# Layer 3's experts by slots: results written straight to the tokens' places, weights kept, weights spread by exact products

## The chip, the core and the metric

The kernel runs on one NeuronCore of a Trainium2 chip, as one launch. The metric is the device time of the launch in microseconds. Five engines work side by side, each through its own instructions in order: TensorE (PE in the profile; its weight loads are PEld), VectorE (DVE), ScalarE (ACT), GpSimd (POOL) and SyncE (SP), which here only issues DMA transfers. POOL issues DMA transfers too: those that cast, and the indirect ones, in which every row has an index of its own.

## The reference, cut to what matters

A decoder of four layers runs on `x` of shape (4, 512, 128). Each layer has an attention, a cross attention over 77 context rows, and a feed-forward part. The change lies in the last part, layer 3's mixture of experts:

```
logits = X @ gate_w.T;  scores = sigmoid(logits)
idx = top_k(scores + bias, 4);  w = scores[idx] / sum
pos = running count of each expert's tokens, over all tokens in order
valid = pos < 128                      # C = 2 * 512 * 4 // 32
xe[expert, pos] = X                    # 32 experts x 128 slots
ye = (silu(xe @ W1) * (xe @ W3)) @ W2  # 128 -> 64 -> 128
out = sum over the 4 choices of ye[expert, pos] * w   (0 where not valid)
out = out + (silu(X @ sw1.T) * (X @ sw3.T)) @ sw2.T   # a shared expert
x = x + out
```

Each expert has 128 slots in all. A token that comes after its expert is full gets nothing from it.

## The kernel before

`x` stays in SBUF as 16 tiles of 128 tokens by 128 channels, four tiles a batch, with `xn` (normalized rows) and `xT` (normalized, channels by tokens). Stages are Python generators. `weave` steps a dense stage and, between its steps, a second chain; the framework then orders each engine's instructions and adds the semaphores. Pools give tiles; a tile with `bufs=n` has n buffers, and the writer of the next one waits until the readers of the one n before are done. PSUM has eight banks, shared out by `banks(...)`: in the last stage four `f`, one `acc`, three `s`.

Layer 3's end, in the order of the program:

- **The cross attention** (`l3_xattn`, 32 items of a batch and a pair of heads) goes through `lagged`: in a round each phase works on another item (projections, scores, values, turn). The softmax division is a POOL operation (L527). Woven into it are the norms and, for batches 0 to 2, `route_slots`: `capped` routes and counts places; from that come `to` (the slot of each token and choice, or a number out of range), `back` (the same, clamped to 0 or more) and `wk` (the weight). Sixteen indirect DMAs a batch on POOL (L749) then write the token's `xn` rows to `slots` in DRAM, 32 x 128 rows of 128 channels, cleared beforehand (`empty_slots`). POOL works in order, so a softmax division behind them waits.
- **The shared expert** of batches 0 to 2 (`shared_rows`).
- **The rounds** (`slot_experts`): eight rounds of four experts. All eight slot tiles are fetched by SP at once (L782), as soon as the last slot write has landed. A round turns the slots (`turn`), multiplies gate and up (`inner`), turns the inner rows (`inner_turn`) and multiplies down (`down`). PSUM is copied to `made` (three buffers; ScalarE L827, VectorE L828), which SP writes to DRAM (L829).
- Beside these, batch 3 is normalized and routed by `route_dense`. `spread` turns its weights and writes them to DRAM as `l_ffn_w`.
- **The dense block** (`ffn` for batch 3): 17 units (the shared expert, then 16 pairs of experts with 64 inner channels each). A unit is gate and up (PE L417, two banks `f`), silu on ScalarE (L939), `h` times up and `h` times the spread weight `c` on VectorE (L428), and down (PE L947), issued two units later and summed in `acc`. `c` is read back from `l_ffn_w` by SP, each row broadcast to 64 partitions (L911).
- **The gathers** (`gathered`), woven into the dense block: 48 indirect DMAs on POOL (L860), 16 a batch, each reading 128 rows of `made` by `back`; VectorE adds each, times `wk`, to `x` (L866); `store` writes the batch out.
- The dense sum is turned and added to `x`, and batch 3 is written out.

The experts' weights are six packs of up to three units, cast while loaded, from POOL (L369). They pass through `feed`, a list of packs for the kernel's four weight buffers (`want(i)` loads up to entry i); the rounds and the dense block each load all six.

Of the kernel before, what the change touches and what calls it, by code (L numbers as in the profile page):

```python
# [130 lines left out]
def pack_all(inp):  # L131
# [6 lines left out]
    p.add("tri4", rep((np.arange(4)[None, :] < np.arange(4)[:, None]).astype(f32)))  # L138
    p.add("slot1", rep((np.arange(32) * CAP + 1).astype(f32)))
# [149 lines left out]
class Net:  # L289
# [7 lines left out]
    def __init__(self, ctx, tc, packs, dram, feed):  # L297
        self.tc, self.nc = tc, tc.nc
        self.packs, self.dram = packs, dram
        self.feed, self.loaded = feed, []  # L300
        self.turn = 0
# [75 lines left out]
    def pack(self, i, name):  # L377
        assert self.feed[i] == name, (self.feed[i], name)
        self.want(i)
        return self.loaded[i]  # L380
# [23 lines left out]
    def lagged(self, items, *phases):  # L404

        for r in range(len(items) + max(lag for _, lag in phases)):
            for phase, lag in phases:
                if 0 <= r - lag < len(items):
                    phase(*items[r - lag])
            yield  # L410
# [298 lines left out]
    def route_dense(self, b, W, pool):  # L709

        m = {}
        yield from self.capped(b, W, pool, m)
        yield
        yield from self.spread(m["w"], (b,), self.weights_in("l3_ffn", 32), pool)

    def route_slots(self, b, W, pool):
# [18 lines left out]
        to, back, none = own([P, TB, K], I32, "to"), own([P, TB, K], I32, "back"), one([P, TB, K], "none")  # L735
        nc.vector.tensor_scalar(none, top, 0.0, 2.0 * E * CAP, ALU.is_equal, ALU.mult)
        nc.vector.scalar_tensor_tensor(to, top, -1.0, none, ALU.add, ALU.add)
        nc.vector.tensor_scalar(back, top, -1.0, 0.0, ALU.add, ALU.max)
        yield
        same, wk = one([P, TB, K, E], "same"), own([P, TB, K], F32, "wk")  # L740
# [3 lines left out]
        nc.vector.tensor_reduce(wk, same, AX.X, ALU.add)  # L744
        self.placed[b] = back, wk
        for t in range(TB):
            for k in range(K):

                put = nc.gpsimd.indirect_dma_start(  # L749
                    out=self.slots, out_offset=bass.IndirectOffsetOnAxis(ap=to[:, t, k : k + 1], axis=0),  # L750
                    in_=self.xn[:, TB * b + t, :], in_offset=None, bounds_check=E * CAP - 1, oob_is_err=False,
                )
                self.tc.declare_no_dep(put.ins, group="slots", reason="rows of their own")
                self.tc.add_to_no_dep_group("slots", put.ins)
            yield

    def empty_slots(self, pool):

        E = 32
        self.slots = self.away.tile([E * CAP, D], F32, name="slots")  # L760
        self.made = self.away.tile([E * CAP, D], F32, name="made")
        self.placed = {}
        none = pool.tile([P, 8 * D], F32, name="none", bufs=1)
        self.nc.gpsimd.memset(none, 0.0)
        rows = self.slots.rearrange("(g p n) d -> g p (n d)", p=P, n=8)
        for g in range(4):
            self.nc.sync.dma_start(rows[g], none)

    def slot_experts(self, base, pool):
# [7 lines left out]
        back = self.made.rearrange("(e c) d -> c e d", c=CAP)  # L777
        xs, st = {}, {}

        def fetch(q):  # L780
            xs[q] = pool.tile([P, 4, D], F32, tag="slots", name="slots", bufs=8)
            nc.sync.dma_start(xs[q], by_expert[:, 4 * q : 4 * q + 4, :])  # L782

        def turn(q):
            t = self.bank("f", (P, 4, P))
            for e in range(4):
                nc.tensor.transpose(t[:, e, :], xs[q][:, e, :], self.ident)
# [4 lines left out]
        def inner(q):  # L792
            ps = self.bank("f", (P, 4, 2, H))
            xT = st.pop((q, "xT"))
            for e in range(4):
# [6 lines left out]
                if e == 3:  # L802
                    self.want(base + i + 2)
# [5 lines left out]
        def inner_turn(q):  # L809
            h = st.pop((q, "h"))  # L810
            t = self.bank("s", (P, 2, P))
# [6 lines left out]
        def down(q):  # L818
# [8 lines left out]
            nc.scalar.copy(y[:, :, 0, :], ps[0])  # L827
            nc.vector.tensor_copy(y[:, :, 1, :], ps[1])  # L828
            nc.sync.dma_start(back[:, 4 * q : 4 * q + 4, :], y.rearrange("p k h d -> p (k h) d"))  # L829
# [4 lines left out]
        yield from self.lagged([(q,) for q in range(8)], (inner, 1), (down, 3), (inner_turn, 2), (turn, 0))  # L834

# [17 lines left out]
    def gathered(self, b, pool):  # L853

        nc = self.nc
        back, wk = self.placed.pop(b)
        for t in range(TB):
            g = pool.tile([P, 4, D], F32, tag="back", name="back", bufs=8)
            for k in range(4):
                nc.gpsimd.indirect_dma_start(  # L860
                    out=g[:, k, :], out_offset=None, in_=self.made,
                    in_offset=bass.IndirectOffsetOnAxis(ap=back[:, t, k : k + 1], axis=0),
                )
            x = self.x[:, TB * b + t, :]
            for k in range(4):
                nc.vector.scalar_tensor_tensor(x, g[:, k, :], wk[:, t, k : k + 1], x, ALU.mult, ALU.add)  # L866
            yield
        self.store(b)
# [23 lines left out]
    def ffn(self, stage, group, E, base, pool):  # L892
# [5 lines left out]
        away = self.chunks[stage]  # L898
# [3 lines left out]
        def chunk():  # L902

            if not rest:
# [16 lines left out]
        for k, blk in enumerate(blocks):  # L921
# [3 lines left out]
            for b in group:  # L925
# [4 lines left out]
                acc = {}  # L930
                for i, (W, u, in_c) in enumerate(plan):
                    if in_c == 0:
                        chunk()
                        c = coming.pop(0)
# [6 lines left out]
                    if in_c is not None:  # L941
                        self.tt(h, h, c[:, in_c, :], ALU.mult)
# [1163 lines left out]
def build(nc, packs, dram):  # L2106
# [5 lines left out]
    for name, part in (  # L2112
        ("l0a", of("l0_ffn")), ("l0b", of("l0_ffn")), ("l1a", of("l1_ffn")), ("l1b", of("l1_ffn")),
        ("l2", f2 + f2), ("x3", ["l3_xattn.q"]), ("l3a", of("l3_ffn")), ("l3b", of("l3_ffn")),
# [3 lines left out]
    with tile.TileContext(nc) as tc, ExitStack() as ctx:  # L2118
# [133 lines left out]
        net.weave(some(steps, 12), chained(net.norm(1), net.norm(2), net.norm(3)), 1)  # L2252
        net.weave(some(steps, 8), chain5(0), 0.41)
        net.want(at["l3a"] + 1)
        net.weave(some(steps, 8), chain5(1), 0.41)
        net.weave(steps, chain5(2), 0.41)
# [6 lines left out]
        banks(f=4, acc=1, s=3)  # L2263
        chain = chained(net.norm(3), net.route_dense(3, W5, s5))
# [29 lines left out]
```

## Time and profile before

| what | value |
|---|---|
| time, median of 3 runs | 2357.78 us (2355.03 to 2363.65) |
| time of the profiled execution | 2353.91 us |
| its span, first to last instruction | 2352.1 us |
| mean granted TensorE clock | 0.96 |
| busy: PE, DVE, ACT, POOL | 2192.3, 1605.1, 1034.3, 572.7 us |
| slot writes `slots<-xn` (POOL), first to last issue | 2102.2 to 2209.5 us |
| slot fetches (SP) | from 2211.6 us |
| gathers `back<-made` (POOL), first to last issue | 2256.6 to 2329.1 us |
| last operation on `x` (DVE) | 2348.0 us |

Positions are microseconds from the start of the span. A timeline line has start, duration, engine, source line, operation, what it writes and reads, and in brackets the idle time before it with what released it; several like operations in a row are one line with xN. An fp32 product over 512 columns stands as two MATMUL records. A line of waits has who waited, for whom, the sum in us, how many times, and the longest. A line of windows has the stretch, its length, each engine's busy time with its instructions, the granted clock as a share, the DMA engines' share and GB/s. Most small helpers carry one source line for all their callers (L417 every product, L428 every two-operand VectorE operation), so the tile's name tells more than the line.

### The profile page before, as it was taken

What the parts mean: (1) busy time and instruction counts of PE and PEld (TensorE: products, weight loads), DVE (VectorE), ACT (ScalarE), POOL (GpSimd) and SP (SyncE); (2) the same over time, 40 slices, a digit from 0 to 9 for tenths busy, and PEclk for the clock granted to TensorE, in tenths of its full rate; (3) what the DMA queues carried; (4) which work ended last, traced back from release to release, by engine and by line L of the source; (5) the groups of instructions that cost most, each with busy time, mean ns of one, the idle gap of its engine ahead of it and who ended that gap; (6) DMA issues with size and microseconds to landing.
All of it is one profiled execution on the core that took longest, in us unless ns stands there. A gap on an engine that the chain in (4) does not pass through costs nothing.

```text
span 2352.1 us, 28673 instructions
## 1 busy us (share of the span) xinstructions
PE 2192.3 (93%) x9282; PEld 1156.3 (49%) x9282; DVE 1605.1 (68%) x4051; ACT 1034.3 (44%) x2105; POOL 572.7 (24%) x712
## 2 busy tenths in 40 slices
PE   6999899999999998999999999999999985999865
PEld 3566556555545453444444444444444443666531
DVE  6677574766766687878777787767767756776433
ACT  4555546434335543444444434444444443455310
POOL 1000001000000103333323333323333322346343
PEclk8998999999999999999999999999999997999887
DMA  5321242354353342333333334333333360000287
GB/s 165 95 69 32 85 124 78 87 131 114 95 148 80 100 104 74 83 92 89 106 91 83 107 104 107 101 91 96 106 91 82 99 127 36 1 6 1 72 161 71
DMA packets 84144, 210.95 MB, mean 90 GB/s; under 512 B 18873, under 2 KB 41721, under 8 KB 83661
## 3 DMA queue, kind: packets, MB, share of 16 engines
q1 hardware_dynamic: 79050, 198.99, 32.0%
q0 software_dynamic: 4944, 10.14, 3.6%
q8 instruction: 73, 1.20, 0.2%
q14 instruction: 77, 0.63, 0.1%
HBM read 179.76 MB, written 20.23 MB: 85 GB/s over the span
## 4 chain that ended last, share of the span: by engine, by line
PE 74%; DVE 13%; issue 4%; DMA 3%; POOL 3%; ACT 2%; another core or an unknown queue 0%; SPq 0%; POOLq 0%; ACTq 0%; DVEq 0%
PE mm L417 21%; PE f L417 12%; PE mm L1783 8%; PE s L417 8%; PE acc L947 5%; PE mm L1750 5%; PE mm L1733 4%; DMA back<-made,back 3%; PE acc L2077 2%; DVE h L428 2%; PE mm L1115 1%; PE mm L1137 1%; DVE m L1077 1%; PE mm L1070 1%; PE s L507 1%
## 5 line engine op out<-in xcount | busy, mean ns | idle before, releaser
L1694 POOL TENSOR_TENSOR gvx<-gvx 128x512 f32<-128x512 f32 (+1 forms) x256 | 260.1, 1016 | 583.1 <-DVE gvx L428 527.9
L417 PE MATMUL f<-xT,w_l_ffn 128*128 128x512 f32 (+1 forms) x768 | 374.9, 610 | 13.4 <-DVE h L428 12.7
L417 PE MATMUL mm<-w_l_ffn_qkv,xT 128*128 128x512 f32 x512 | 265.4, 603 | 3.3 <-DVE roped L1665 1.7
L1814 ACT ACTIVATE at_e<-mm,at_m 128x512 f32<-128x512 f32 x256 | 173.0, 685 | 215.1 <-DVE at_m L1812 209.3
L1783 PE MATMUL mm<-og,w_l_ffn_o 128*128 128x512 f32 x512 | 264.6, 600 | 0.0
L939 ACT ACTIVATE h<-f 128x512 f32<-128x512 f32 x189 | 112.5, 596 | 289.3 <-PE f L417 253.4
L947 PE MATMUL acc<-h,w_l_ffn 128*128 128x512 f32 x378 | 200.5, 616 | 30.1 <-issue 10.3
L417 PEld LDWEIGHTS f<-xT,w_l_ffn 128*128 128x128 f32 (+1 forms) x768 | 141.5, 194 | 168.9 <-issue 130.0
L428 DVE TENSOR_TENSOR h<-h,f 128x512 f32<-128x512 f32 (+1 forms) x192 | 131.4, 686 | 130.4 <-PE f L417 99.2
L428 DVE TENSOR_TENSOR og<-mm,c 128x512 f32<-128x512 f32 x256 | 175.9, 688 | 29.0 <-PE mm L1783 27.6
L428 DVE TENSOR_TENSOR gvx<-mm,gv 128x512 f32<-128x512 f32 x256 | 174.4, 683 | 23.6 <-PE mm L417 18.9
L1734 ACT COPY eT<-mm 128x512 f32<-128x512 f32 x256 | 137.7, 595 | 72.9 <-PE mm L1733 72.6
L1812 DVE TENSOR_REDUCE at_m<-mm 128x1 f32<-128x512 f32 x256 | 161.2, 683 | 8.7 <-PE mm L417 7.0
L1733 PEld LDWEIGHTS mm<-ident,at_e 128*128 128x128 f32 x1024 | 120.0, 141 | 67.0 <-issue 49.4
L1783 PEld LDWEIGHTS mm<-og,w_l_ffn_o 128*128 128x128 f32 x512 | 89.4, 191 | 97.0 <-issue 85.3
L1733 PE MATMUL mm<-ident,at_e 128*128 128x128 f32 x1024 | 134.1, 273 | 2.6 <-ACT at_e L1814 2.6
L417 PE MATMUL mm<-roped 64*128 64x512 f32 x512 | 133.3, 623 | 1.5 <-DVE roped L428 1.0
L947 PEld LDWEIGHTS acc<-h,w_l_ffn 128*128 128x128 f32 x378 | 71.6, 196 | 125.5 <-issue 81.4
L417 PEld LDWEIGHTS mm<-w_l_ffn_qkv,xT 128*128 128x128 f32 x512 | 86.7, 190 | 91.9 <-issue 69.4
L1077 DVE TENSOR_REDUCE m<-mm 128x1 f32<-128x512 f32 (+3 forms) x176 | 105.2, 637 | 31.9 <-PE mm L1073 31.0
L428 DVE TENSOR_TENSOR h<-h,c 128x512 f32<-128x512 f32 x176 | 121.4, 696 | 4.2 <-DMA c<-l_ffn_w 1.1
L1750 PE MATMUL mm<-eT,v 128*64 128x512 f32 x512 | 119.5, 599 | 0.0
(440 smaller groups left out, 3672.1 us busy)
## 6 DMA issues: line engine op xcount, KB each, us to landing
c<-gates SPq DMA_DIRECT2D x256, 256.0 KB
c<-l_ffn_w SPq DMA_DIRECT2D x106, 384.0 KB
w_l_ffn<-in_l_ffn SPq DMA_DIRECT2D x26, 576.0 KB
w_l_ffn_qkv<-in_l_ffn_qkv SPq DMA_DIRECT2D x16, 640.0 KB
w_l_ffn_o<-in_l_ffn_o SPq DMA_DIRECT2D x16, 512.0 KB
rot<-qk SPq DMA_DIRECT2D x128, 64.0 KB
w_l_ffn<-in_l_ffn POOLq DMA_DIRECT2D x10, 576.0 KB
k_parts<-k SPq DMA_DIRECT2D x12, 384.0 KB
```

Source lines behind the costliest of these rows:

```text
L417: self.nc.tensor.matmul(out, lhsT=lhsT, rhs=rhs, start=i == 0, stop=i == len(pairs) - 1)
L428: self.nc.vector.tensor_tensor(out, a, b, op)
L939: nc.scalar.activation(h, pg, AF.Silu)
L947: nc.tensor.matmul(acc["t"], lhsT=W["d" + u], rhs=h, start=i == 0, stop=i == n - 1)
L1077: nc.vector.tensor_reduce(m[:, i, h0 : h0 + per], ps, AX.X, ALU.max, negate=True)
L1694: nc.gpsimd.tensor_tensor(x[:, :, :m], x[:, :, :m], x[:, :, m : 2 * m], ALU.add)
L1733: nc.tensor.transpose(p[:, j, :], es[i][hl][:, j * P : j * P + P], self.ident)
L1734: nc.scalar.copy(eT[hl][:, :, i * P : i * P + P], p)
L1750: nc.tensor.matmul(po[64 * hl : 64 * hl + 64, :], lhsT=m["v"][:, j, hl, :], rhs=eT[hl][:, j, :], start=j == 0, stop=j == TB - 1,)
L1783: nc.tensor.matmul(acc, lhsT=W["o"][:, (e - 1) * D : e * D], rhs=hs.pop(e - 1), start=e == 1, stop=e == E)
L1812: nc.vector.tensor_reduce(m, s, AX.X, ALU.max, negate=True)
L1814: nc.scalar.activation(e[:, :n], s, AF.Exp, bias=m, accum_out=den)
```

## The change

- A slot row has 130 columns: the token's row, its weight, and its place (token times 4 plus choice) as an integer. `sent` (one buffer) is filled by ScalarE copies, a VectorE reduction (the weight) and an addition (the place), and the 16 indirect writes a batch send its rows. Unused slots carry weight 0 and a place out of range.
- In a round, the down results are multiplied by the slots' weight as they leave PSUM (two operations on each of ScalarE and VectorE instead of one), and four indirect DMAs on POOL write them to the tokens' places in `back` (6144 rows in DRAM, cleared beforehand). Instead of the 48 gathers, `returned` reads one block a batch by SP and adds four operands of 128x512 to `x`.
- Batch 3's weights are split into three bf16 parts whose sum is the fp32 value, turned, and kept in SBUF (`w3T`). Each unit's spread weight is a bf16 product of `pick3`, zeros and ones, with `w3T` into an `s` bank (`spread3`), which VectorE reads in place of `c`. No DRAM round trip is left.
- The six weight packs are loaded once: three through the feed, three into the last stage's pool (`stay`).
- `inner_turn` takes an `f` bank instead of an `s` bank. `lagged` yields after each phase instead of each round, and the weaves' paces are changed to match. In the dense block VectorE keeps the program's order.

```diff
@@ lagged
                     phase(*items[r - lag])
-            yield
+                    yield
@@ route_dense
-        yield from self.spread(m["w"], (b,), self.weights_in("l3_ffn", 32), pool)
+        w3, rest = pool.tile([P, TB, 3, E], BF16, ...), pool.tile([P, TB, E], F32, ...)
+        nc.vector.tensor_copy(w3[:, :, 0], m["w"])
+        self.tt(rest, m["w"], w3[:, :, 0], ALU.subtract)
+        nc.vector.tensor_copy(w3[:, :, 1], rest)
+        self.tt(w3[:, :, 2], rest, w3[:, :, 1], ALU.subtract)
+        yield
+        t = self.bank("s", [3 * E, S], BF16)
+        for j in range(TB):
+            nc.tensor.transpose(t[:, j * P : j * P + P], w3[:, j].rearrange("p k e -> p (k e)"), self.identb)
+        self.w3T = pool.tile([3 * E, S], BF16, name="w3T", bufs=1)
+        nc.scalar.copy(self.w3T, t)
@@ route_slots
-        nc.vector.tensor_scalar(back, top, -1.0, 0.0, ALU.add, ALU.max)
+        sent = pool.tile([P, TB, K, D + 2], F32, name="sent", tag="sent", bufs=1)
+        for t in range(TB):
+            nc.scalar.copy(sent[:, t, :, :D], self.xn[:, TB * b + t, :].unsqueeze(1).to_broadcast([P, K, D]))
+        nc.vector.tensor_scalar(
+            sent[:, :, :, D + 1].bitcast(I32), self.const["place"].rearrange("p (t k) -> p t k", k=K),
+            float(b * S * K), None, ALU.add,
+        )
...
-        nc.vector.tensor_reduce(wk, same, AX.X, ALU.add)
-        self.placed[b] = back, wk
+        nc.vector.tensor_reduce(sent[:, :, :, D], same, AX.X, ALU.add)
...
-                    in_=self.xn[:, TB * b + t, :], in_offset=None, ...
+                    in_=sent[:, t, k, :], in_offset=None, ...
@@ empty_slots
+        self.back = self.away.tile([3 * S * K, D], F32, name="back")
+        rows = pool.tile([3 * E, E], F32, name="own_rows", bufs=1)
+        self.pick3 = pool.tile([3 * E, E, 64], BF16, name="pick3", bufs=1)
...
+        self.nc.gpsimd.tensor_copy(self.pick3, rows.unsqueeze(2).to_broadcast([3 * E, E, 64]))
...
+        nowhere = none[:, :, D + 1]
+        self.nc.vector.tensor_scalar(nowhere.bitcast(I32), nowhere, float(1 << 20), None, ALU.add)
...
+        for g in range(6):
+            self.nc.sync.dma_start(rows[g], zero)
@@ slot_experts
-            t = self.bank("s", (P, 2, P))
+            t = self.bank("f", (P, 2, P))
...
-            nc.scalar.copy(y[:, :, 0, :], ps[0])
-            nc.vector.tensor_copy(y[:, :, 1, :], ps[1])
-            nc.sync.dma_start(back[:, 4 * q : 4 * q + 4, :], y.rearrange("p k h d -> p (k h) d"))
+            for k in range(2):
+                w = [xs[q][:, 2 * k + half, D : D + 1] for half in range(2)]
+                nc.scalar.activation(y[:, k, 0, :], ps[0][:, k, :], AF.Copy, scale=w[0])
+                nc.vector.tensor_scalar(y[:, k, 1, :], ps[1][:, k, :], w[1], None, ALU.mult)
+                for half in range(2):
+                    self.alone("back", nc.gpsimd.indirect_dma_start(
+                        out=self.back, in_=y[:, k, half, :], in_offset=None,
+                        out_offset=bass.IndirectOffsetOnAxis(
+                            ap=xs[q][:, 2 * k + half, D + 1 : D + 2].bitcast(I32), axis=0
+                        ),
+                        bounds_check=3 * S * 4 - 1, oob_is_err=False,
+                    ))
...
+    def spread3(self, units):
+        out = {}
+        for u in units:
+            out[u] = self.bank("s", (P, S))
+            at = 2 * int(u)
+            self.dot(out[u], (self.pick3[:, at : at + 2, :].rearrange("r e i -> r (e i)"), self.w3T))
+        return out
@@ gathered -> returned
+        for b in batches:
+            rows[b] = pool.tile([P, TB, 4, D], F32, name=f"back{b}", bufs=1)
+            src = self.back[b * S * 4 : (b + 1) * S * 4].rearrange("(t p k) d -> p t k d", p=P, k=4)
+            self.nc.sync.dma_start(rows[b], src)
+        yield
+        for b in batches:
+            x = self.rows_of(self.x, b)
+            for k in range(4):
+                self.tt(x, x, rows[b][:, :, k, :], ALU.add)
+                if k % 2:
+                    yield
+            self.store(b)
@@ ffn
+                    if in_c is not None and spread:
+                        if u not in cs:
+                            cs.update(spread([v for _, v, in_c in plan[i : i + 2] if in_c is not None]))
+                        cu = cs.pop(u)
...
-                        self.tt(h, h, c[:, in_c, :], ALU.mult)
+                        self.tt(h, h, cu, ALU.mult)
@@ build
-        net.weave(some(steps, 8), chain5(0), 0.41)
-        net.want(at["l3a"] + 1)
-        net.weave(some(steps, 8), chain5(1), 0.41)
-        net.weave(steps, chain5(2), 0.41)
+        net.weave(some(steps, 32), chain5(0), 1.7)
+        net.want(at["l3"] + 1)
+        net.weave(some(steps, 32), chain5(1), 1.7)
+        net.weave(steps, chain5(2), 1.15)
...
+        net.want(at["l3"] + 2)
+        for i, n in enumerate(of("l3_ffn")):
+            net.stay[n] = net.loaded[at["l3"] + i] if i < 3 else net.load(n, ff, f"w{i}")
...
-        net.weave(chained(shared, net.slot_experts(at["l3a"], ff)), chain, 1.2)
-        back = chained(*[net.gathered(b, ff) for b in range(3)])
-        net.weave(net.ffn("l3_ffn", (3,), 32, at["l3b"], ff), back, 1, 2)
+        net.weave(chained(shared, net.slot_experts(at["l3"], ff)), chain, 2.2)
+        with tc.manual_schedule(engines={mybir.EngineType.DVE}):
+            back = net.returned(range(3), ff)
+            next(back)
+            net.weave(net.ffn("l3_ffn", (3,), 32, at["l3"], ff, net.spread3), back, 1.5, 6)
```

## The prediction

> **What bounds the kernel now.** I read first where the span has holes, then what ends last, then each hole's releaser. The page's slices (58.8 us each):
>
> ```profile
> PE   6999899999999998999999999999999985999865
> ...
> PEclk8998999999999999999999999999999997999887
> DMA  5321242354353342333333334333333360000287
> ```
>
> TensorE is full almost everywhere; the last two slices (2234 to 2352) hold 6 and 5 tenths at a lowered clock, while the DMA engines, idle before, go to 8 and 7 tenths. The change works only in the last 340 us. The waits in 2250:2341 say what the holes are:
>
> ```profile
> ACT h L939 <- PE f L417: 63.1, 12, 15.5
> DVE x L866 <- DMA back<-made,back: 54.2, 30, 11.9
> ```
>
> ScalarE's 63.1 us only follow TensorE. VectorE waits 54.2 us for gathered rows, 30 times. It works in program order, so each wait also holds the dense block's `h` products behind it, and TensorE for free banks. The chain of waits cut to 2240:2352.1 puts 54.4% on "DMA back<-made,back". How fast the dense block goes when fed shows in TensorE's timeline:
>
> ```profile
> 2291.74 1.02 PE L947 MATMUL acc<-h,w_l_ffn 128*128 128x512 f32 x2
> 2292.60 1.88 PE L417 MATMUL f<-xT,w_l_ffn 128*128 128x512 f32 x4
> 2294.32 1.02 PE L947 MATMUL acc<-h,w_l_ffn 128*128 128x512 f32 x2
> 2295.18 1.88 PE L417 MATMUL f<-xT,w_l_ffn 128*128 128x512 f32 x4
> ```
>
> From one `acc` to the next is 2294.32 - 2291.74 = 2.58 us: 1.72 for gate and up, 0.86 for down. Seventeen units are 43.9 us, yet the block runs from about 2249 to 2346. So half of it is waiting.
>
> Why are gathers slow and index writes not? The DMA answer for 2189:2211 holds 16 writes `slots<-xn`:
>
> ```profile
> DMA packets 481, 0.03 MB, mean 1 GB/s; under 512 B 480, under 2 KB 480, under 8 KB 480
> ```
>
> Sixteen writes of 128 rows by 512 B would be 1.05 MB; 0.03 went. Nearly all rows were out of range (their experts' 128 slots were already full) and cost the DMA nothing. A gather cannot skip: `back` is clamped to row 0 or more. In 2320:2330 the engines are 97% busy at 66 GB/s. The 48 gathers take from 2256.6 to about 2341, 1.76 us each.
>
> **Part by part.**
>
> *Gathers go* (L860, L866): 48 x 0.98 us on POOL, 48 x 0.35 us on VectorE, and the waits. *The spread of batch 3's weights goes:* the chain has the write of `l_ffn_w` (2249.48 to 2253.41), SP's issue (0.46) and 2.72 for `c`; with it go twelve transfers `c` and the eight writes of `made` from SP. In its place stand four small VectorE operations (0.2 to 0.3 us by `wf` and cast rows), four bf16 transposes (0.23) and one copy (0.57), all issued among the rounds: nothing on the path. *Weights stay:* the old second load goes, six loads. The three new pool tiles are issued on POOL behind batch 2's writes (order of instructions) and share DMA with the slot fetch, which moves 2.11 MB by about 2220; three loads at some 2 us of all engines end near 2227, and the first is needed at round 3 (2229 before). Zero, at most 3.
>
> *Spread products come:* 16 bf16 matmuls of 512 columns. Bounds: 0.22 (half of the fp32 product's two 0.43 records) to 0.50 (the old `mm<-turned,pick` row). I take 0.25, since the block is warm when fed: a unit is 2.83 us.
>
> *`sent` and the slots' rows:* three times four ScalarE copies of 128x512, 0.6 us each (the `xT` row), 2.4 per batch; ScalarE is under half busy there (9.51 of 20 in 2100:2120). The first must wait for all 16 writes of the batch before (one buffer), and ScalarE's `xT`, `q`, exponentials and `eT` queue behind it, and so TensorE. In time before, batch 0's writes leave POOL at 2125.2 and `xT` comes at 2128.2; batch 1's at 2170.6 and 2173.6: about 3 us of cover. If it goes, ScalarE stands for what is late: three writes are 3.8 us, so up to 4 us per batch. The first write now also needs the weights' sum:
>
> ```profile
> 2189.52 0.17 DVE L737 SCALAR_TENSOR_TENSOR to<-m,none 128x16 int32<-128x16 f32 x1
> 2189.64 0.69 DVE L428 TENSOR_TENSOR same<-same,wf 128x512 f32<-128x512 f32 x1
> 2190.37 0.69 DVE L744 TENSOR_REDUCE wk<-same 128x16 f32<-128x512 f32 x1
> ```
>
> 2191.06 instead of 2189.69, for batch 2, whose 16 writes end the stage: +1.4. I put +1.5 on everything after. The finer weave of this stage (a step per phase) has the same total; it can win back at most the 7 us that TensorE idles in 2080:2180, or lose as much. I take zero. The new POOL work of the clearing (two memsets of 0.97, one bf16 copy, between 0.6 and 4.2 us by the `pick` and `kb` rows) falls in POOL's hole from 1959 to 1990, the six more clears in an idle DMA.
>
> *The rounds.* `made` becomes two smaller operations on each engine: VectorE +0.28 per round (0.35 row), ScalarE +0.45 (0.41, `xn` row); both have over 1 us free per 3.3 us round. New on POOL are 32 index writes. Their price by the nearest rows:
>
> ```profile
> 2206.90 0.97 POOL L749 DMA_INDIRECT slots<-xn,to  x1 [0.30 <-issue]
> 2208.18 0.97 POOL L749 DMA_INDIRECT slots<-xn,to  x1 [0.30 <-issue]
> 2209.46 0.97 POOL L749 DMA_INDIRECT slots<-xn,to  x1 [0.30 <-issue]
> ...
> 2211.60 5.49 SPq L782 DMA_DIRECT2D slots<-slots  x8
> ```
>
> (The last line is SP's view.) 1.27 us apart, the last landed 1.17 us after POOL let go. Low end 1.27, high end 1.76, the gathers' pace. I take 1.27: unused slots carry a place out of range, so again nearly nothing moves. Four per round are 5.1 us against TensorE's 3.3: **POOL becomes the pace of the rounds**, though TensorE need not follow until `made` (three buffers) runs out. First `made` 2227.6 + 1.5 = 2229. Round 7's `made` needs round 4's writes: 2229.3 + 20 x 1.27 + 1.2 = 2256, against 2249.4 + 1.5. By the order of instructions the dense block's second spread product takes the bank that round 7's ScalarE copy frees, and VectorE's `h` stands behind the same `made`. So TensorE stops from about 2251 to 2256 with only unit 0's products done.
>
> [...] The same 0.97 + 0.30 stand in 2100:2120 (VectorE 17.15 of 20 busy) and in 2200:2210 (1.37 of 10). [...] I go by the row.
>
> **The sum,** on the profiled execution (span 2352.1, time 2353.91). From 2256 sixteen units remain, with two downs behind the last up: 16 x 2.83 - 1.7 = 43.6. An idle of 5 us lowers the clock: 2210:2220, after 4.57 us idle, shows 0.60. I add 2 us. Last up at 2301.6. From the last up to the end it was 2352.1 - 2342.7 = 9.4: end at 2311. **The span falls by 41 us**, the time to 2313. The median is 3.9 above the profiled execution, so the median would be 2317; I say 2315.
>
> What is late next is the returned rows: last write 2229.3 + 32 x 1.27 + 1.2 = 2271; three reads of 1.05 MB, 4 to 7 us each at the slot fetch's 150 to 250 GB/s: 2277, 2282, 2288. Batch 0's adds stand behind unit 7's `h` (2276): a wait of 1 us. VectorE needs 1.38 of each 2.83 us unit, so 12 adds of 0.69 fit in nine units. Cover for both ends; without it the adds cost 8.3.
>
> **Rivals.**
> 1. *The hold is smaller.* The bank order lets TensorE go on, and the clock stays: 5 + 2 us less, 2308; with the finer weave winning up to 7, 2301. For: TensorE runs ahead in this trace. Against: the order of instructions. 0.2.
> 2. *The writes or the `xn` copies cost more.* At 1.76 per write the block starts 9.8 later and the adds wait another 3; with 4 us twice from `sent` behind late writes, 2315 + 13 to 2315 + 21. For: real bytes in the rows that are used. Against: the 0.03 MB. 0.22.
> 3. *Slower than before:* the return writes themselves become the gathers' heir. The price p per write decides, through the reads that wait for all 32: last write 2229.3 + 32p + 1.2, first read 6, then VectorE's nine units and twelve adds (20.7) and a tail of 6. That passes 2352 at p = 2.8. At p = 3.0 it ends at 2359, time 2361. For: the same queue waited 13 us for gathers at its end. Against: no index write in the trace takes over 1.31 us. 0.04.
> 4. *It does not do what it says:* writes do not run beside the rounds but behind them all, with the dense block held until the last: 2271 instead of 2256, 2330. 0.04, counted in the range.
>
> The forecast's own case, 2308 to 2322, has 0.5. **Range** 2300 to 2336: from rival 1 with the weave's gain to rival 2's far end. **Chances:** about 0.5% (12 us) is what a measurement can tell from no change; faster 0.93, within 0.03, slower 0.04.
>
> **What would show it.** Right: no wait of VectorE for `back` over a few us; the last index write near 2271; `made` of rounds 6 and 7 waiting for a DMA; dense units 2.8 us apart from about 2256; end near 2311. Wrong: index writes over 1.4 us apart; TensorE waiting on spread banks in every unit (two of three `s` banks per pair); ScalarE idle before `sent` in the attention stage; adds on `x` late.

## The result, and the profile after

| | before | changed |
|---|---|---|
| median, 12 runs each | 2352.86 us (2351.05 to 2364.51) | 2357.23 us (2351.16 to 2368.51) |
| time of the profiled execution | 2353.91 us | 2354.23 us |
| its span | 2352.1 us | 2352.4 us |
| first slot write to slot fetch | 109.4 us | 132.5 us |
| slot fetch to the end of the span | 140.5 us | 112.8 us |

The ratio is 1.001, with a 95% interval of 0.9996 to 1.0025: no change that can be measured, where 2315 us was predicted. One plain warning belongs here: some groups of runs that stood together shared a condition in which the end of the program is 15 to 20 us longer for kernels with index writes; the changed kernel's own profile has it, and the runs are told in groups below for that reason.

The last rows of the table are the result in short. The end of the program gained 27.7 us, and the attention stage gave 23.1 of them back. (The rest of the 27.9 us by which the fetch comes later stands ahead of the first slot write, which came at 2107.0 instead of 2102.2.)

The page's slices after, to be laid beside those of before:

```profile
PE   6999999999999998999999999999999984997678
...
PEclk7998999999999999999999999999999997997869
DMA  5321342344353432333333333333333361000022
```

The gathers' traffic is gone: the last two digits of the DMA line were 8 and 7 and are now 2 and 2. TensorE's last two slices are 7 and 8 tenths instead of 6 and 5. But the two ahead of them (2117 to 2235, the attention stage) have fallen from 9 and 8 to 7 and 6, and the clock in the last but one, which holds the rounds, from 8 tenths to 6.

The waits of the attention stage (2095 to 2240), the first three lines:

```profile
ACT sm_e L2120 <- DVE sm_e L432: 47.0, 14, 15.5
POOL sm_e L531 <- DVE sm_s L530: 29.4, 11, 4.6
DVE sent L759 <- DMA slots<-sent,to: 28.2, 2, 14.2
```

Before, in 2095 to 2212, the first of these was far shorter:

```profile
ACT sm_e L2059 <- DVE sm_e L428: 14.0, 10, 1.8
```

The third line of the changed kernel is the place to look, and e1 and e2 below test it: VectorE waits twice, 14 us each, for the index writes into `slots`. Its timeline and ScalarE's at that place:

```profile
2131.23 0.18 DVE L759 TENSOR_SCALAR sent<-w_const 128x16 int32<-128x16 f32 x1 [14.17 <-DMA slots<-sent,to]
2131.31 0.17 DVE L480 BATCH_NORM_AGGREGATE mv<-st 128x2 f32<-128x6 f32 x1
```

```profile
2133.36 0.84 ACT L2120 ACTIVATE sm_e<-sm_e 128x308 f32<-128x308 f32 x2 [15.54 <-DVE sm_e L432]
```

L759 is the addition that puts the tokens' places into `sent`. It takes 0.18 us and reads nothing but a constant. It stood in VectorE's order between two operations of the norm (the next line is the norm's), so it came up for batch 1 while batch 0's writes were still leaving POOL, and all of VectorE's softmax work stood behind it. The windows of these two waits and of the stretches after them show what TensorE did meanwhile (columns: stretch, its length, busy time of PE, PEld, DVE, ACT and POOL with instructions, the clock, DMA share, GB/s):

```profile
2101.20:2131.20 30.00, 20.93 (x105) 13.64 (x104) 13.37 (x47) 9.51 (x19) 20.84 (x24) 0.90 0.04 10
2131.20:2145.00 13.80, 8.99 (x28) 6.33 (x29) 8.29 (x30) 7.79 (x16) 2.75 (x4) 0.50 0.00 1
2161.50:2191.50 30.00, 21.25 (x108) 13.96 (x107) 13.38 (x47) 9.51 (x19) 20.85 (x24) 0.92 0.02 1
2191.50:2205.00 13.50, 8.90 (x40) 6.69 (x41) 8.75 (x43) 9.29 (x18) 2.41 (x5) 0.67 0.00 1
```

In each of the two 30 us that end with a wait TensorE is idle for 9 us (30.00 less 20.93, and less 21.25), and the stretches after them run at 0.50 and 0.67 of the clock.

In the last part, 2250 to 2352, the waits are these (the first lines, and one further down):

```profile
ACT h L1000 <- PE f L421: 29.5, 13, 6.4
POOL back L868 <- ACT made L865: 23.7, 4, 15.0
...
ACT slotsT L827 <- remote: 6.4, 1, 6.4
```

The 54.2 us that VectorE waited for gathered rows have gone, and the 63.1 of `h` are 29.5. The chain of waits from 2240 has 3.5% on the index writes where 54.4% lay on the gathers; the rest is mostly TensorE's own products. "Remote" is a wait whose end the profile can't put down to an instruction.

The index writes began as predicted, 15.5 us after the fetch, and stood some 1.3 us apart:

```profile
2255.05 1.04 POOL L868 DMA_INDIRECT back<-made,slots  x1 [14.99 <-ACT made L865]
2256.39 1.00 POOL L868 DMA_INDIRECT back<-made,slots  x1 [0.30 <-issue]
2257.70 0.97 POOL L868 DMA_INDIRECT back<-made,slots  x1 [0.31 <-issue]
...
2267.29 0.97 POOL L868 DMA_INDIRECT back<-made,slots  x1 [2.24 <-ACT made L865]
```

But POOL then waited for `made`: 2.24 us at 2267.29, and more later. The 32 writes took 49.5 us instead of 32 x 1.27 = 40.6. Of the 2.1 MB that they could carry they moved 0.28 MB: four writes sent their whole 64 KB and the others next to nothing, as the prediction had it. So what 32 writes with all rows in range would cost is not shown here. The dense block, once it is fed, has the predicted pace:

```profile
2308.10 1.02 PE L1008 MATMUL acc<-h,w_l_ffn 128*128 128x512 f32 x2
...
2310.67 1.02 PE L1008 MATMUL acc<-h,w_l_ffn 128*128 128x512 f32 x2
...
2313.68 1.02 PE L1008 MATMUL acc<-h,w_l_ffn 128*128 128x512 f32 x2
...
2316.26 1.02 PE L1008 MATMUL acc<-h,w_l_ffn 128*128 128x512 f32 x2
```

2.57, 3.01, 2.58: 2.79 us a unit over pairs, 2.83 predicted. A spread product costs 0.22.

### The profile page after: what moved, and what is told of

The parts are those of the page before. It is cut to its first block, busy times and chain, and to the rows that moved or that the text cites. A ratio compares the mean times of both kernels' runs of the same rounds, so it can differ in the third digit from the quotient of the medians.

```text
span 2352.4 us, 28695 instructions
## 1 busy us (share of the span) xinstructions
PE 2200.4 (94%) x9298; PEld 1165.8 (50%) x9298; DVE 1604.9 (68%) x4027; ACT 1041.3 (44%) x2126; POOL 555.5 (24%) x693
## 5 line engine op out<-in xcount | busy, mean ns | idle before, releaser
L432 DVE TENSOR_TENSOR h<-h,f 128x512 f32<-128x512 f32 (+1 forms) x192 | 131.1, 684 | 146.0 <-PE f L421 110.9
L432 DVE TENSOR_TENSOR og<-mm,c 128x512 f32<-128x512 f32 x256 | 175.3, 686 | 29.1 <-PE mm L1844 27.7
L1844 PEld LDWEIGHTS mm<-og,w_l_ffn_o 128*128 128x128 f32 x512 | 90.0, 192 | 97.6 <-issue 85.8
L432 DVE TENSOR_TENSOR h<-h,c 128x512 f32<-128x512 f32 x160 | 110.4, 695 | 3.9 <-DMA c<-l_ffn_w 1.0
```

The lines of the kernel that those rows point to most:

```text
L432: self.nc.vector.tensor_tensor(out, a, b, op)
L1844: nc.tensor.matmul(acc, lhsT=W["o"][:, (e - 1) * D : e * D], rhs=hs.pop(e - 1), start=e == 1, stop=e == E)
```

## The experiments

The measures used for all runs are two stretches of the profiled execution: **attention**, from the first slot write to the slot fetch (POOL's first `slots<-...` line to SP's fetch), and **end**, from the slot fetch to the end of the span. They leave out the stages before, whose length differs by up to 18 us between executions (the first slot write stands at 2102.2 to 2120.3 us). Runs of one letter stood side by side on one chip. The ratio is to the kernel before in that group.

| run | group | attention | end | median | ratio (95%) |
|---|---|---|---|---|---|
| before (its profile) | | 109.4 | 140.5 | 2352.86 | |
| changed (its profile) | | 132.5 | 112.8 | 2357.23 | 1.001 (0.9996 to 1.0025) |
| e1 three `sent` | A | 110.9 | 115.7 | 2338.85 | 0.9928 (0.9903 to 0.9953) |
| e2 late place | A | 114.0 | 113.6 | 2337.49 | 0.9914 (0.9889 to 0.9940) |
| e3 three `sent`, eight `made` | A | 111.0 | 115.6 | 2340.96 | 0.9931 (0.9907 to 0.9954) |
| e4 no return writes | A | 111.1 | 92.4 | 2312.10 | 0.9814 (0.9786 to 0.9843) |
| e5 rows by SP | B | 111.1 | 92.3 | 2314.28 | 0.9812 (0.9794 to 0.9829) |
| e6 rows by POOL | B | 111.0 | 92.4 | 2316.45 | 0.9811 (0.9793 to 0.9828) |
| e7 POOL busy | B | 110.9 | 95.9 | 2317.33 | 0.9822 (0.9806 to 0.9838) |
| e8 three `sent`, old weave | B | 113.9 | 97.5 | 2321.28 | 0.9855 (0.9815 to 0.9895) |
| e9 three `sent` | C | 111.2 | 97.1 | 2317.90 | 0.9833 (0.9817 to 0.9850) |
| e10 old weave | C | 114.1 | 97.6 | 2327.74 | 0.9861 (0.9838 to 0.9884) |
| e11 old weave in the rounds | C | 111.1 | 96.4 | 2317.72 | 0.9827 (0.9808 to 0.9847) |
| e12 old weave in the attention | C | 113.9 | 98.4 | 2321.81 | 0.9854 (0.9835 to 0.9874) |
| e13 changed | D | 134.4 | 111.1 | 2358.13 | 0.9996 (0.9976 to 1.0016) |
| e14 late place | D | 118.1 | 112.3 | 2343.20 | 0.9937 (0.9917 to 0.9956) |
| e15 three `sent` | D | 111.3 | 113.3 | 2336.66 | 0.9914 (0.9887 to 0.9940) |
| e16 no return writes | D | 111.3 | 92.5 | 2315.72 | 0.9831 (0.9804 to 0.9858) |
| e17 rows by POOL | E | 110.9 | 92.2 | 2313.48 | 0.9826 (0.9809 to 0.9842) |
| e18 changed | E | 134.4 | 95.2 | 2343.03 | 0.9951 (0.9935 to 0.9968) |

The kernel before had medians of 2358.1, 2360.0, 2357.5, 2359.1 and 2356.1 us in groups A to E.

### Is it the one buffer, or the order? (e1, e2)

My theory after the result: the place addition (L759), early in VectorE's order, waits for the batch before's writes. Rivals: the finer weave made the stage longer, or POOL's writes are the chain whatever VectorE does.

e1:

```diff
-        sent = pool.tile([P, TB, K, D + 2], F32, name="sent", tag="sent", bufs=1)
+        sent = pool.tile([P, TB, K, D + 2], F32, name="sent", tag="sent", bufs=3)
```

> The changed kernel with three buffers of `sent` instead of one; nothing else. Theory A (VectorE's addition of the place, L759, which needs only a constant, stands early in VectorE's order and waits for the batch before's 16 slot writes): both waits of 14.2 and 14.0 us go, the slot fetch comes 25 to 28 us earlier (about 2212 instead of 2239.6), and the time falls by about as much, to about 2327. Theory B (the finer weave and its paces made the attention stage longer): the waits go, but other idle time takes their place; the fetch moves by less than 8 us and the time stays above 2344. Theory C (POOL's slot writes are themselves the chain): the fetch moves by less than 8 us, with POOL busy or waiting in every stretch.

e2, with the one buffer kept:

```diff
+        late = one([P, TB, K], "late")
+        nc.vector.tensor_scalar(late, top, 0.0, None, ALU.mult)
-        nc.vector.tensor_scalar(sent[...], place, float(b * S * K), None, ALU.add)
+        nc.vector.scalar_tensor_tensor(sent[...], place, float(b * S * K), late, ALU.add, ALU.add)
```

> The changed kernel with its one buffer of `sent`, but the addition of the place also adds a zero made from the batch's own top choices, so that it can't stand early in VectorE's order; one small VectorE operation more per batch. If the ORDER is the cause, not the buffer: nearly all of what three buffers give, the fetch near 2212 to 2218 and the time 2327 to 2333, with ScalarE's copies into `sent` waiting 0 to 3 us per batch. If one buffer is too few wherever the operation stands: a wait of 8 us or more moves to ScalarE's copies, and the time stays above 2342.

Both waits of VectorE went, and the attention stretch fell from 132.5 to 110.9 us in e1, within 2 us of the kernel before. The addition in e1, with no wait in front of it:

```profile
2124.32 0.33 DVE L759 TENSOR_SCALAR sent<-w_const 128x16 int32<-128x16 f32 x1
```

So one buffer of `sent`, as VectorE's order used it, costs 21.6 us. (In groups D and E the changed kernel has 134.4, so 23.) e2 says how much of it is the order alone: 114.0, so 18.5 of the 21.6 come back with the single buffer, as the theory had it. The weave and POOL's chain fall as rivals for these 21 us. In e2 the wait that the prediction had named is left. ScalarE's timeline:

```profile
2127.60 0.45 ACT L2122 ACTIVATE sm_e<-sm_e 128x308 f32<-128x308 f32 x1
2133.23 0.62 ACT L758 COPY sent<-xn 128x512 f32<-128x512 f32 x1 [5.18 <-issue]
2133.75 0.58 ACT L512 COPY xT<-s 128x512 f32<-128x512 f32 x1
```

The copy into `sent` stands idle for 5.18 us, and `xT` behind it. The view names no releaser ("issue"), but in the trace's instructions ScalarE waits there for the semaphores of the batch before's writes until 2132.96, and the last of these left POOL at 2130.83 + 0.97. This is the prediction's "up to 4 us per batch", real and a little longer, but small beside VectorE's 14.

The times fell less than expected, to 2339 and 2337 instead of about 2327. In e1 the end stretch was 115.7 us, where the prediction had 2311 - 2213.1 = 97.9. So a second loss of some 18 us was in the rounds and what follows them.

### What slows the rounds? (e3 to e7)

e3 takes away the wait for buffers of `made` (`bufs=3` to `bufs=8`, with three of `sent`); e4 the return writes themselves.

> Three buffers of `sent`, and `made` with eight buffers instead of three, so that no round waits for the return writes of an earlier one. If the buffers of `made` hold the rounds (the prediction's hold of 5 us, plus its lowered clock): 5 to 9 us less than with three buffers of `sent` alone. If the rounds are slow because TensorE runs them at half clock after a gap, whatever POOL does: within 3 us of it; VectorE and ScalarE then still wait for TensorE in rounds 3 to 7.

> Three buffers of `sent`, and the 32 return writes of the rounds left out (so the rows of the experts are never returned: part of the computation is left out). It gives the price of the writes. If they set the pace of the rounds: the dense block starts 10 us or more earlier than with them, and the time is 8 to 15 us below that of three buffers of `sent` alone. If they lie beside the rounds: within 3 us of it, and the slow rounds have another cause.

Eight buffers changed nothing (115.6 against 115.7): the prediction's hold is not where these 18 us went. Without index writes it is 92.4 us. So in group A the writes cost 23 us, far more than the 5 us of hold and 2 for the clock that the prediction drew from POOL's pace.

Three replacements were to say what in a write does it, all with three buffers of `sent` and eight of `made`. In e5 SP issues plain transfers of the same pieces, in e6 POOL does, in e7 POOL computes instead:

```diff
-                    self.alone("back", nc.gpsimd.indirect_dma_start(out=self.back, in_=y[:, k, half, :], ...))
+                    at = (4 * q + 2 * k + half) * P
+                    nc.sync.dma_start(self.back[at : at + P], y[:, k, half, :])
```

(e6 has `nc.gpsimd` for `nc.sync`), and in e7:

```diff
-                    self.alone("back", nc.gpsimd.indirect_dma_start(out=self.back, in_=y[:, k, half, :], ...))
+                    wide = y[:, k, half, :].unsqueeze(1).to_broadcast([P, 4, D])
+                    nc.gpsimd.tensor_tensor(own, wide, wide, ALU.add)
```

> Three buffers of `sent`, eight of `made`, and in the place of the 32 index writes of the rounds 32 plain transfers of the same 128x128 pieces, issued by SP to rows in order (the places of the tokens are left out). All bytes move, 2.1 MB, where the index writes move nearly nothing. From the slot fetch to the end it was 115.7 us with the index writes and 92.4 us with no writes. Theory P (what costs the 23 us is on POOL's side of an index write): 92 to 96 us from fetch to end. Theory D (it is the traffic or the completion of many small transfers beside the rounds, whoever issues them): 105 us or more.

> The same with the 32 plain transfers issued by POOL instead of SP, without indices. Fetch to end near 115 us: it is POOL's way of issuing a transfer, with or without indices. Near 93 us: it is the index (the row of indices read, the rows skipped). In between: by POOL's time per write, which the trace then shows.

> The 32 index writes replaced by 32 POOL additions of 128x512 into a tile that nobody reads (1.0 us each by the 128x512 rows on POOL, as long as a write's 0.97); no transfer in the rounds (the return of the rows is left out). If POOL being busy and reading and writing SBUF beside VectorE is the cost: fetch to end 105 us or more. If not: 92 to 96 us, as with no writes.

92.3, 92.4 and 95.9: none of them costs what the index writes cost in A (POOL's additions 3.5 us, against the 92.4 of e4). Taken alone this would have convicted the index. But a fourth kernel of the same group had the index writes.

### The weave, and a story that fell (e8 to e12)

e8 puts the old weave back (a yield per round of phases, the old paces), with three buffers of `sent`:

```diff
                     phase(*items[r - lag])
-                    yield
+            yield
```

> Three buffers of `sent` with the weave of the kernel before (a yield per round of phases, its four paces in the attention stage and its pace in the rounds). If the finer weave is worth something: from the first slot write to the slot fetch longer than the 110.9 us measured with three buffers alone, by up to the 7 us that the prediction allowed; if it costs: shorter. I expect 109 to 114 us there, and a time within 8 us of the kernel with three buffers (2338.9).

It took 97.5 us at the end, with all 32 index writes. Either the old weave frees the rounds, or group B differs from group A. So the same kernels once more, with both halves of the weave, in one group:

> The kernel with three buffers of `sent` once more, beside the three that follow, so that all four stand on one chip. If its slow rounds (115.7 us from slot fetch to end) are of the kernel: again 113 to 117 us and a time of 2335 to 2342. If they are of the chip or of the moment: 96 to 100 us from fetch to end, as the old weave had, and about 2320.

> Three buffers of `sent` and the old weave once more. If the weave is what frees the index writes from their 20 us: again 97 to 98 us from fetch to end, 2320, below the kernel beside it by 15 us or more. If chip or moment did it: no difference over 5 us between the two.

> Three buffers of `sent`; the attention stage woven as in the changed kernel, the rounds as in the kernel before (a yield per round, pace 1.2: batch 3's routing products stand one round later). If it is the rounds' own order that matters: 97 to 99 us from fetch to end. If not: 113 to 117.

> The other half: the attention stage woven as in the kernel before, the rounds as in the changed kernel. The opposite of the run before it, if the cause lies in the order at all: 113 to 117 us from fetch to end when the rounds' order matters, 97 to 99 when something of the attention stage (what is still under way when the rounds begin) does.

The very kernel that had taken 115.7 us in e1 took 97.1 in e9, and its median fell from 2338.85 to 2317.90. All four lie between 96.4 and 98.4. The weave as the cause of the slow rounds is out; what it is worth shows in the attention stretch: 111.1 and 111.2 with the new one, 113.9 and 114.1 with the old. The finer weave gains 2.8 us there; in the end stretch nothing shows (the old rounds are 0.7 and 0.8 us shorter, one execution each). By the time, e10 is 9.8 us above e9 where less than 5 was expected. Its profiled execution (2333.86 us) lost them ahead of the two stretches: ScalarE's first `q` of the cross attention stands at 2036.80 us, against 2023.43 in e9.

ScalarE's timeline from the fifth `slotsT` of the eight says what differs. First e1, then e9:

```profile
2240.22 0.59 ACT L827 COPY slotsT<-f 128x512 f32<-128x512 f32 x1 [1.55 <-PE f L825]
2245.17 0.38 ACT L841 ACTIVATE inner<-f 128x256 f32<-128x256 f32 x1 [4.36 <-remote]
```

```profile
2239.32 0.59 ACT L827 COPY slotsT<-f 128x512 f32<-128x512 f32 x1 [0.24 <-PE f L825]
2241.17 0.38 ACT L841 ACTIVATE inner<-f 128x256 f32<-128x256 f32 x1 [1.26 <-PE f L421]
```

In e1 ScalarE stands idle for 4.36 us. The products that it waits for are in the records, the last ending at 2242.02. By the trace's updates of the semaphore on which ScalarE waits for them, TensorE tells of these products only at 2245.14, and then of five groups of products within 0.21 us (2245.14 to 2245.35). TensorE's own records go on to 2243.46 meanwhile:

```profile
2242.86 0.60 PE L825 MATMUL f<-ident,slots 128*128 128x128 f32 x4
2246.91 0.79 PE L421 MATMUL s<-w_l_ffn,innerT 64*128 64x128 f32 x2 [3.45 <-DVE innerT L851]
```

So it had work, and its word came late; it then stands idle itself for what VectorE makes of that word. Windows from 20 us after the fetch, three of 10 us each, e1 and then e9:

```profile
2236.50:2246.50 10.00, 5.40 (x44) 4.25 (x43) 2.19 (x8) 2.93 (x8) 6.13 (x7) 1.00 0.06 17
2246.50:2256.50 10.00, 8.83 (x38) 7.75 (x38) 1.68 (x6) 1.05 (x4) 7.37 (x8) 0.52 0.02 0
2256.50:2266.50 10.00, 8.54 (x40) 7.05 (x41) 3.05 (x10) 3.04 (x7) 3.43 (x4) 0.50 0.03 7
```

```profile
2236.80:2246.80 10.00, 9.34 (x76) 7.90 (x77) 3.48 (x11) 4.20 (x11) 7.73 (x8) 1.00 0.07 17
2246.80:2256.80 10.00, 9.33 (x70) 6.83 (x69) 5.44 (x18) 4.87 (x12) 7.70 (x8) 1.00 0.03 2
2256.80:2266.80 10.00, 6.84 (x17) 3.08 (x16) 2.67 (x5) 1.82 (x4) 7.57 (x9) 0.83 0.04 8
```

The order of the two ills is in the first row of each. At full clock TensorE is busy for 5.40 us instead of 9.34: the late word comes first. Then the clock falls to half for 23.9 us, by the trace's clock records. In the second row TensorE is busy for 8.83 us with 38 products, where it did 70 in 9.33. Late words go on meanwhile: the copy at 2257.49 waited for products whose records end at 2255.74 and whose updates stand at 2257.36 and 2257.42. How much of the 18 us is the late words' and how much the clock's, and whether the gaps of the one keep the other down, no run separates.

### Kernel, chip or moment? (e13 to e18)

The changed kernel itself, with the two cures of `sent` and without writes, in one group:

> The changed kernel itself, unaltered. If the slow rounds belong to the place and moment of a run: 96 to 99 us from slot fetch to end on a chip where the version with three buffers takes 97, a time of 2336 to 2342, and the two waits of 14 us of VectorE are all that is lost against three buffers. If they belong to one buffer (the rounds begin with TensorE at half clock after a longer idle): 111 to 114 us again, and 2352 to 2358, wherever it runs.

> The late place with one buffer, beside the changed kernel and the three buffers. By the first runs it gives back 18 of the 22 us in the stretch from the first slot write to the fetch: 113 to 116 us there (132.5 in the changed kernel, 111 with three buffers), a time 2 to 6 us above three buffers.

> Three buffers of `sent` a third time, as the measure for the two above and the one below: 2316 to 2320 where the rounds are undisturbed, 2335 to 2342 where they are not.

> Three buffers and no return writes (the rows of the experts aren't returned: part of the computation is left out), on the same chip. If the index writes cost what the undisturbed runs say: 4 to 6 us less than three buffers with writes, since the dense block then need not wait for POOL's 32 writes. If 20 us or more: the writes disturb the rounds on this chip too.

Group D was like A: 111 to 113 us with index writes, 92.5 without. Side by side, three buffers are worth 2358.13 - 2336.66 = 21.5 us, the late place 2358.13 - 2343.20 = 14.9, which is 6.5 behind three buffers where 2 to 6 was expected. The late place's attention stretch was 118.1 this time, above the 113 to 116 that I expected. ScalarE's copies into `sent` show no wait there; by the semaphore updates TensorE's word came 2 to 3 us late (at 2133.7, 2173 and 2184.8), as it did in e2 at 2121.7. So 114.0 and 118.1, both from disturbed groups, may be more than the late place costs by itself; it never ran in an undisturbed one.

> Plain POOL transfers of the rows in place of the index writes (the places of the tokens are left out), three buffers of `sent`. The kind of chip is read from the trace (TensorE's semaphore updates are recorded in full, or some 20 of 2,815 are missing) and from the kernel beside it. On a chip that slows the index writes: 92 to 96 us from fetch to end if the index is what disturbs, 105 or more if any transfer of POOL's does. On a chip that does not: 92 to 93 again, which adds nothing.

> The changed kernel itself, unaltered. On a chip that slows the index writes: 111 to 113 us from fetch to end and 2352 to 2358, as twice before. On a chip that does not: 96 to 99 us, a time of 2336 to 2342, all of the loss left being the two waits of 14 us.

Group E stood on the same chip as A by the chip number on record (6), and it was not like A. The changed kernel took 95.2 us at the end, 134.4 in the attention, and 2343.03 in all; the ratio, 0.9951 (0.9935 to 0.9968), is about a half per cent faster than before. So, unless that number stands for two chips, the slow rounds are not of the chip, and they are not of the kernel alone: without index writes the end was not longer in the disturbed groups either (92.4 and 92.5 us in e4 and e16), and with them it hangs on something that a group of runs has or lacks. One mark of it is in the traces. In A and D, and in the two profiles of before and changed, some of TensorE's semaphore updates are missing from the records (2,788 of 2,815 in e1, 2,795 of 2,814 in the changed kernel's profile, also 2,798 of 2,815 in e4, which isn't slow). In B, C and E none is. The late words keep to the same runs: three or more of TensorE's updates in a row, each within 0.08 us of the next, stand once to five times in every profile of A and D and three times in the changed kernel's own, always after 2130 us, and never in B, C or E or in the profile before.

That is as far as the runs go. Every run here was recorded, so they can't tell whether the late words are TensorE's own or come of the recording. e17 fell into a group of the undisturbed kind (92.2 us), and so had e5, e6 and e7. So neither plain transfers, by POOL or by SP, nor a busy POOL were ever tried in a disturbed group: whether it is the index, any transfer, or POOL at work beside the rounds stays open.

## Why the prediction was wrong

**The step that failed** is the part "*`sent` and the slots' rows*". It said that the copies of ScalarE must wait for the 16 writes of the batch before, that there are about 3 us of cover, and that it costs up to 4 us per batch if the cover goes. It asked only about ScalarE's copies. The same buffer has three writers, and the one with the shortest work, VectorE's place addition, needs no data but a constant; nothing kept it behind the norm. VectorE works in its program's order, so while this addition waited for the buffer (14.17 us), everything behind it waited too (the norm's next operation came at 2131.31). The order of instructions had it: it stands there between two operations of the norm, with a wait for eight DMA semaphores. The prediction put this wait at nothing. The sum with the measured size, on e18's profiled execution, in a group without the late words:

- predicted fetch 2213.1, measured 2238.8: +25.7. The first write stands 2.2 later than before (2104.4), the single buffer takes 23.2 (134.4 against 111.2 in e9), the rest of the stage 1.8 (111.2 against 109.4); less the 1.5 that were predicted.
- predicted 97.9 us from fetch to end, measured 95.2: -2.7.
- 2311 + 25.7 - 2.7 = 2334.0, the span of e18.

In the changed kernel's own profile it is 2311 + 26.5 + 14.9 = 2352.4: the same error of the fetch, and from the fetch to the end 14.9 us more than predicted, in disturbed rounds, which no step of the prediction had and whose cause stays open. The first error alone would have put the time out of the range: e18's median is 2343.03 us.

**The terms that held**, by e9 and e18, with the predicted value first:

- First return write after the fetch: 16 us; 17.3 in e9 and 15.4 in e18.
- Index writes at 1.27 us: 40.7 us for 32 of them in both, without a gap. The row of 0.97 and 0.30 was right; VectorE beside them (5.44 of 10 busy in e9) did not slow them. The price of 1.76 and rival 3's 2.8 fall, for writes of which four in 32 move rows.
- The hold of TensorE behind `made` and the spread banks, 5 us, and 2 for the clock: 3.15 us in e9 and 3.32 in e18, and in each one stretch of 3.4 us at half clock. The second spread product stands 44.7 and 42.8 us after the fetch, where the prediction had the block go on at 2256 - 2213.1 = 42.9. Against e5's 92.3 us (eight buffers of `made`) the writes and their hold cost 4.8 us in e9 and, in e5's own group, 5.2 in e8. TensorE's timeline in e9:

```profile
2257.95 0.39 PE L421 MATMUL s<-w3T,pick 96*128 96x512 bf16 x1
2261.50 0.59 PE L421 MATMUL s<-w3T,pick 96*128 96x512 bf16 x1 [3.15 <-ACT made L865]
```

- Dense unit 2.83: 2.79. Spread product 0.25: 0.22.
- The adds of returned rows, covered: the first stands at 2282.37 in e9 and at 2302.46 in e18, with no wait for the rows.
- The finer weave, zero within 7 us: a gain of 2.8.
- Tail after the last up, 9.4: about 8 in e9.

**The rivals.** The first (a smaller hold) was right in its part, 3.15 for 5, and hidden in the time by the other errors. The second came nearest by its mechanism, `sent` behind late writes, but on ScalarE and for 4 us: with the order mended, e2 shows that wait at 5.18. The fourth (writes not beside the rounds) fell: they ran beside them. Nothing in the range of 2300 to 2336 stood for VectorE's wait, and the chance of 0.03 for no change was far too small.

**A version that beats both.** With three buffers of `sent` and nothing else changed, e9 took 2317.90 us, a ratio of 0.9833 (0.9817 to 0.9850), and in the disturbed groups 0.9928 and 0.9914; beside the changed kernel itself, in group D, it is 21.5 us faster. In an undisturbed group that is within 3 us of the predicted 2315, with the failed step taken out.

## What to carry to other kernels

When an edit puts a tile with one buffer between two engines, list every writer of that tile, not only the large one, and look up in the order of instructions where each stands. Here the smallest, which depends on a constant, was put early, and then held its whole engine until the buffer was free. Another buffer gave back 21 to 23 us of that stretch, and an operand that makes the small operation late 16 to 19. And before a loss is put down to an edit, run the same kernel again beside its variants: here a difference of 18 us, with a good story in its trace, was of the group of runs and not of the weave.

## What the runs showed of the hardware that was not expected

- In e1 TensorE's completions became known 1.6 and 3.1 us after its records end (updates at 2257.36 and 2245.14 for products to 2255.74 and 2242.02), five groups of products within 0.21 us (2245.14 to 2245.35). Such updates in a row were seen in groups A and D and in the changed kernel's own profile alone (there from 2240.84, 2266.35 and 2306.06 us). Without index writes in the rounds (e4, e16) one group of three stands just after the fetch and the end was not longer (92.4 and 92.5 us). In the attention stage it cost nothing with three buffers (110.9 to 111.3 us in every group) and was clear with the late place (2 to 3 us at a time in e14, whose stretch took 118.1 us). Whether it comes of the recording is open.
- In disturbed rounds the clock stayed at half for 23.9 us on end in e1 and 27.3 in the changed kernel's profile, by the trace's clock records, against 3.4 us in e9 after a wait of 3.15. Small products alone did not hold it there: the rounds begin at half clock in e1 and in e9 alike (17.1 us) and come back to full within them (1.00 in the 10 us from 20 us after the fetch, in both).
- In undisturbed groups a plain transfer of 128x128 issued by POOL or SP in place of an index write cost nothing that shows: 92.4 and 92.3 us at the end (eight buffers of `made`), against 92.4 with no transfers at all (e4, in group A).
